# Splitting fp32 operands for one-pass matmuls: upper parts made by ScalarE instead of a VectorE mask, operands in dense blocks

## The chip, the cores and the metric

The kernel runs on one core of a Trainium2 chip. The metric is the device time of one launch in microseconds; lower is better. The core's engines are called as in the profile: PE is TensorE (PEld its weight loads), DVE is VectorE, ACT is ScalarE, POOL is GpSimd, SP is SyncE, which issues nearly all transfers.

## The reference

Four graph layers run over `x` (32 graphs of 512 nodes with 128 features) with one adjacency matrix `adj` (512 x 512) for all graphs. Each layer takes a layer norm with a relu of `x` and adds its result to `x`.

```python
h = relu(layernorm(x)); x = x + L0(h)     # graph convolution: (D^-1/2 (adj+I) D^-1/2) h W^T + b
h = relu(layernorm(x)); x = x + L1(h)     # gated graph network, five steps
h = relu(layernorm(x)); x = x + L2(h)     # graph attention, elu
h = relu(layernorm(x)); x = x + L3(h)     # graph attention

def L1_step(h):                           # in_matrix = out_matrix = adj
    m = adj @ h
    av = concat(m, m)
    z = sigmoid(av @ w3^T + h @ u3^T + b)
    r = sigmoid(av @ w4^T + h @ u3^T + b)
    hv = tanh(av @ w5^T + (r * h) @ u5^T + b)
    return (1 - z) * h + z * hv
```

The inputs and the output are fp32.

## The kernel before

**Tiling.** A graph is held as tiles of 128 partitions by 4 x 128 values: nodes on partitions in four chunks of 128 (`C = 4`), or features on partitions. Matmuls contract over partitions in chunks of 128, and products with `adj` have 512 columns.

**Products in three parts.** A matmul with fp32 operands takes two passes here (the profile counts two PE instructions for one). Products with the adjacency matrix in the gated steps (`adj`) and in most of the graph convolutions (`an`, the normalized matrix) use instead the type `float32r`, which takes one pass[...]. `in_three` splits the operand `h` in an upper part and a lower part and makes a third, `across`, from both; `factors_of` does so once for the matrix. Three one-pass products then stand for one in fp32: upper by upper and lower by lower in one PSUM bank, then a scale of the bank by 1 + 1/4096 on ACT (L630), then across by across on top (four matmuls each, L623), and a copy of the bank to `m` on ACT (L632). There are 188 such products: 160 with `adj` and 28 with `an`.

In the kernel before, the upper part begins with `cut`: DVE masks off the low 12 bits of `h` as an int32 (L613; L423 for the matrix). ACT copies `cut` to `upper` in the one-pass type (L615; L425), and DVE makes `lower` (L616; L426) and `across` (L617; L430) from `cut`. For the matrix, ACT also scales `lower` by 4096 (L428), and `across` is made from the scaled part.

**Steps and lanes.** Each graph goes through five gated steps. `step` takes `m` and the transposed state `hT`, makes the gates `r` (L729, L730, then tanh L732), `z` (L736, L738), the candidate (L743, L744, L746) and the new state (L748 to L751). Six graphs, the lanes, are under way at a time.

**Two ways to turn the state.** The new state has features on partitions; the next product needs nodes on partitions. In the first and last part of the program PE transposes it (L576) and ACT copies it (L762). In between (`EARLY <= due < STEPS * B`), `shuttle` does it: DVE transposes blocks of 32 x 32 (L584) into `sq`, four transfers write `sq` to DRAM as `far` (L587), and one reads it back as `h` (L589). In the kernel before, the shuttled state is laid out as `"(j c)"`: the values of one chunk lie four elements apart. `rows` in `in_three` then reads the matmul's weights with that stride where `turned` is true. The last step's result is added to `x` from the same layout (L766). The graphs' input to the attention layers passes through `shuttle` too, in the order `"(c j)"`.

**The order of the work.** Nothing is ordered by hand. Each operation is given to a `Plan` with its engine, an assumed cost in microseconds, a due time, and what it reads and writes. The plan plays the operations through once per trial, with a heap of ready ones for each engine and buffers taken from named pools (eight PSUM banks, two `cut`, two `upper`, two `lower`, three `across`, and so on), keeps the best trial, and emits the instructions of each engine in that order. On the chip each engine then works strictly in the order emitted. The assumed costs are the second argument of `op`, among them `V` for a DVE pass over 512 values, `A` for one on ACT, `MR` = 0.216 for a one-pass matmul of 512 columns. After `IDLE_FROM` the plan puts idle transposes (L321) where PE would rest.

Of the kernel before, what the change touches and what calls it, by code (L numbers as in the profile page):

```python
# [9 lines left out]

F32 = mybir.dt.float32
F32R = mybir.dt.float32r
I32 = mybir.dt.int32
U8 = mybir.dt.uint8
AF = mybir.ActivationFunctionType
ALU = mybir.AluOpType
# [1 line left out]
P = 128  # L18
# [4 lines left out]
Q = P // W  # L23
# [10 lines left out]

SPLIT = 4096.0
UPPER = -4096


class Val:
# [228 lines left out]
def gnn_stack(ctx: ExitStack, tc: tile.TileContext, a: dict, out: bass.AP):  # L270
# [13 lines left out]
    def flat(t):  # L284
# [110 lines left out]
    for c in range(C):  # L395
        p = Val("bank")
        turned.append(p)

        def turn_adj(c=c, p=p):
            for m in range(C):  # L400
                nc.tensor.transpose(p.t[:, m, :], adj_sb.t[:, c, m * P:(m + 1) * P], ident.t)
        op("PE", C * TURN, -800, turn_adj, r=[adj_sb[c], ident], w=[p])
        op("ACT", A, -800, lambda c=c, p=p: nc.scalar.copy(adjT.t[:, :, c * P:(c + 1) * P], p.t), r=[p], w=[adjT[c]])
# [92 lines left out]
    def norm_stats(b, due):  # L496
        xb, st, mv, ve = xs[b], Val("st", C), Val("mv"), Val("ve")
        for c in range(C):
            op("DVE", 0.21, due, lambda c=c: nc.vector.bn_stats(st.t[:, c, :], xb.t[:, c, :]), r=[xb[c]], w=[st[c]])
# [5 lines left out]
        op("DVE", 0.45, due, aggr, r=[st], w=[mv, ve])  # L505
        return mv, ve

    def norm_relu(b, y, due, times=None):
# [68 lines left out]
        op("PE", C * TURN, due, turns, r=[y, ident], w=[p, *then])  # L577
        return p

    def shuttle(src, squares, dst, due, soon, inner="(c j)"):  # L580


        sq, far = Val("sq"), Val("far", Q)
        op("DVE", 0.61, soon, lambda: nc.vector.transpose(  # L584
            sq.t.rearrange(f"p q {inner} -> p q c j", c=C), flat(src.t).rearrange(squares, c=C, q=Q)), r=[src], w=[sq])
        for k in range(Q):
            op("SP", 0.44, due, lambda k=k: nc.sync.dma_start(  # L587
                far.t[:, :, k, :].rearrange("q i f -> i q f"), sq.t[k * W:(k + 1) * W]), r=[sq], w=[far[k]], delay=4)
        op("SP", 0.4, due, lambda: nc.sync.dma_start(dst.t, far.t.rearrange("q i k f -> (q i) k f")), r=[far], w=[dst], delay=5)  # L589

    def shuttle_first(h, hT, due, soon):

        sq, far = Val("sq"), Val("far", Q)
        op("DVE", 0.61, soon, lambda: nc.vector.transpose(
            sq.t.rearrange("p k (c i) -> p k c i", c=C), h.t.rearrange("p c (k j) -> p k c j", k=Q)), r=[h], w=[sq])
        for q in range(Q):
            op("SP", 0.44, due, lambda q=q: nc.sync.dma_start(
                far.t[:, :, q, :].rearrange("k j f -> j k f"), sq.t[q * W:(q + 1) * W]), r=[sq], w=[far[q]], delay=4)
        for q in range(Q):
            op("SP", 0.4, due, lambda q=q: nc.sync.dma_start(  # L600
                hT.t.rearrange("p c (q i) -> q p c i", q=Q)[q], far.t.rearrange("k j q (c i) -> q (k j) c i", c=C)[q]),
               r=[far[q]], w=[hT[q]], delay=5)

    def in_three(h, turned, factors, due):

        cut, upper, lower, across = Val("cut"), Val("upper"), Val("lower"), Val("across")
# [4 lines left out]
        op("DVE", 0.35, due - 5, lambda: nc.vector.tensor_scalar(  # L613
            flat(cut.t).bitcast(I32), flat(h.t).bitcast(I32), UPPER, None, op0=ALU.bitwise_and), r=[h], w=[cut])
        op("ACT", A, due - 5, lambda: nc.scalar.copy(flat(upper.t), flat(cut.t)), r=[cut], w=[upper])  # L615
        op("DVE", V, due - 5, lambda: nc.vector.tensor_sub(flat(lower.t), flat(h.t), flat(cut.t)), r=[h, cut], w=[lower])  # L616
        op("DVE", V, due - 5, lambda: nc.vector.scalar_tensor_tensor(  # L617
            flat(across.t), flat(cut.t), 1 + 1 / SPLIT, flat(h.t), op0=ALU.mult, op1=ALU.subtract), r=[h, cut], w=[across])
        p, m = Val("bank"), Val("m")

        def times(left, right, first):
            for c in range(C):
                nc.tensor.matmul(flat(p.t), rows(left.t, c), right.t[:, c, :], start=first and c == 0, stop=c == C - 1,  # L623
                                 skip_group_check=True)
# [5 lines left out]
        op("ACT", A, due - 6, lambda: nc.scalar.mul(flat(p.t), flat(p.t), 1 + 1 / SPLIT), w=[p])  # L630
        op("PE", 4 * MR, due, lambda: times(across, across_of, False), r=[across, across_of], w=[p, m])
        op("ACT", A, due - 6, lambda: nc.scalar.copy(flat(m.t), flat(p.t)), r=[p], w=[m])  # L632
        return m

    def product(h, due):

        p, m = Val("bank"), Val("m")
        for c in range(C):
# [8 lines left out]
        op("ACT", A, due, lambda: nc.scalar.copy(flat(m.t), flat(p.t)), r=[p], w=[m])  # L647
        return m

    def normalized(begun):  # L650
# [56 lines left out]
    def ggnn(b, due):  # L707
# [4 lines left out]
        if FAR0 <= b < B - FAR1:  # L712
            shuttle_first(h, hT, due - 2.5, due - 3)
        else:
            p = to_features(h, due - 2, hT)
            op("ACT", A, due - 2, lambda hT=hT: nc.scalar.copy(flat(hT.t), flat(p.t)), r=[p], w=[hT])
        turned = False
        for s in range(STEPS):
            now = due + LANES * s
# [5 lines left out]
    def step(b, s, m, hT, due, lane):  # L725
# [30 lines left out]
        if not EARLY <= due < STEPS * B:  # L756
# [2 lines left out]
                op("DVE", V, due + 2, lambda: nc.vector.tensor_add(flat(xs[b].t), flat(xs[b].t), flat(p.t)),  # L759
                   r=[p, lane], w=[xs[b]])  # L760
            else:
                op("ACT", A, due + 1, lambda: nc.scalar.copy(flat(h.t), flat(p.t)), r=[p], w=[h])  # L762
            return h, False, new
        shuttle(new, "p (c q i) -> p q c i", h, due, due - 5, "(j c)")
        if last:
            op("DVE", V, due + 2, lambda: nc.vector.tensor_add(  # L766
                xs[b].t.rearrange("p c (k j) -> p k c j", k=Q), xs[b].t.rearrange("p c (k j) -> p k c j", k=Q),
                h.t.rearrange("p k (j c) -> p k c j", c=C)), r=[h, lane], w=[xs[b]])
        return h, True, new


# [25 lines left out]
    def gat(b, l, due):  # L797
# [4 lines left out]
        if near:  # L802
            rstd, g = center_relu(b, y, due), Val("off", 2)
            pT = to_features(y, due + 1, gT)
            op("ACT", A, due + 1, lambda: nc.scalar.copy(flat(gT.t), flat(pT.t)), r=[pT], w=[gT])
        else:
            norm_relu(b, y, due)
            shuttle(y, "p (c q j) -> p q c j", gT, due + 0.5, due)
# [47 lines left out]
            op("SP", 0.4, due + 1.5, lambda: nc.sync.dma_start(  # L856
                row.t, line.t.rearrange("c q i -> (c q i)").unsqueeze(0).to_broadcast([P, N])), r=[line], w=[row, e], delay=7)
        for j in range(C):
            op("DVE", 0.68, due + 3, lambda j=j: nc.vector.scalar_tensor_tensor(  # L859
                e.t[:, j, :], matrix(row), h.t[:, j, D + 1:D + 2], mask.t[:, j, :], op0=ALU.max, op1=ALU.mult),  # L860
               r=[row, h[2 + j // 2], mask], w=[e[j]])

# [112 lines left out]
```

## Time and profile before

| | us |
|---|---|
| median of 3 runs | 1607.32 (1606.89 to 1607.37) |
| the profiled execution's own time | 1608.62 |
| span of the profiled execution | 1606.8 |
| PE busy | 1589.5 |
| PE weight loads busy (overlap PE) | 1160.8 |
| DVE busy | 1481.0 |
| ACT busy | 905.6 |
| POOL busy | 152.5 |

The span runs from the first to the last instruction on the core; the time of a run has a little around it. Busy times are of one profiled execution. A row of a group gives the line, engine, operation, the tiles out<-in, the shape, the count, then busy microseconds in total and the mean nanoseconds of one, then the idle time of the engine just before those instructions and what ended it.

### The profile page before, as it was taken

To read this page: it belongs to the slowest core of one execution; us is meant where nothing else is said; L and a number is where in the kernel's file an instruction comes from. 1 tells how busy PE (TensorE), PEld (TensorE's weight loads), DVE (VectorE), ACT (ScalarE), POOL (GpSimd) and SP (SyncE) were. 2 spreads that over 40 slices of the span, in tenths; PEclk is the share of its full clock that TensorE was granted. 3 is DMA by queue.
4 is the path that set the end of the run, shared out by engine and by line. 5 is a ranking of instruction groups with operands and counts; after the bars stand their busy time and mean duration, and the time that the engine had idled before them with its cause. 6 is when DMAs were issued, how large, how long until landed. Compare 5 with 4: busy or idle time off the path is not lost.

```text
span 1606.8 us, 23090 instructions
## 1 busy us (share of the span) xinstructions
PE 1589.5 (99%) x6966; PEld 1160.8 (72%) x6966; DVE 1481.0 (92%) x3751; ACT 905.6 (56%) x1822; POOL 152.5 (9%) x137
## 2 busy tenths in 40 slices
PE   8899999999999999999999999999999999999998
PEld 7576667776777776777777686777676766767678
DVE  8989789999999999999999999999999899987888
ACT  6765555555555545645555645655655555555464
POOL 2111000000100101010110110101010000000010
PEclk9999999999999999999999999999999999999999
DMA  3134233444543443444433534444344424432201
GB/s 105 33 86 110 64 95 97 116 115 113 126 103 101 105 119 92 109 114 120 117 100 93 125 102 122 109 102 112 87 124 116 110 71 106 115 100 66 53 27 41
DMA packets 270141, 157.66 MB, mean 98 GB/s; under 512 B 81248, under 2 KB 236224, under 8 KB 270016
## 3 DMA queue, kind: packets, MB, share of 16 engines
q1 hardware_dynamic: 269728, 155.66, 38.0%
q8 instruction: 55, 0.90, 0.2%
q14 instruction: 70, 0.57, 0.1%
q10 hardware_dynamic: 288, 0.52, 0.1%
HBM read 86.25 MB, written 69.84 MB: 97 GB/s over the span
## 4 chain that ended last, share of the span: by engine, by line
PE 90%; DVE 7%; ACT 1%; issue 1%; POOL 0%; DMA 0%; DVEq 0%; ACTq 0%; POOLq 0%
PE bank L623 32%; PE bank L885 11%; PE bank L729 8%; PE bank L730 8%; PE bank L743 8%; PE bank L744 8%; PE bank L736 8%; PE bank L818 3%; PE bank L693 2%; PE bank L871 1%; DVE sq L584 1%; DVE e L859 1%; PE bank L576 0%; DVE hT L751 0%; DVE hv L748 0%
## 5 line engine op out<-in xcount | busy, mean ns | idle before, releaser
L512 POOL TENSOR_TENSOR rstd<-ve,mhalf 128x4 f32<-128x4 f32 x119 | 140.8, 1184 | 1366.1 <-DVE ve L504 1161.8
L885 PEld LDWEIGHTS bank<-h_gat,e 128*128 128x128 f32 x1792 | 210.5, 191 | 17.9 <-issue 14.4
L623 PE MATMUL bank<-adj,across 128*128 128x512 f32 x640 | 215.3, 462 | 1.6 <-ACT bank L630 1.6
L630 ACT ACTIVATE bank<-bank 128x512 f32<-128x512 f32 x188 | 109.3, 581 | 186.2 <-PE bank L623 183.6
L885 PE MATMUL bank<-h_gat,e 128*128 128x129 f32 x1792 | 212.2, 275 | 0.3 <-DVE v L890 0.3
L623 PE MATMUL bank<-adj,upper 128*128 128x512 f32 x640 | 201.2, 436 | 1.3 <-ACT upper L615 1.3
L623 PEld LDWEIGHTS bank<-adj,across 128*128 128x128 f32 x640 | 156.2, 280 | 41.6 <-issue 22.4
L732 ACT ACTIVATE r<-bank,gate_bw 128x512 f32<-128x512 f32 x160 | 109.7, 686 | 127.3 <-PE bank L730 118.4
L623 PE MATMUL bank<-adj,lower 128*128 128x512 f32 x640 | 177.0, 398 | 0.0
L623 PEld LDWEIGHTS bank<-adj,upper 128*128 128x128 f32 x640 | 154.4, 280 | 30.1 <-issue 8.8
L729 PE MATMUL bank<-m,wT 128*128 128x512 f32 x320 | 164.4, 595 | 3.0 <-ACT m L632 2.5
L736 PE MATMUL bank<-m,wT 128*128 128x512 f32 x320 | 163.4, 594 | 1.8 <-ACT r L732 1.8
L743 PE MATMUL bank<-m,wT 128*128 128x512 f32 x320 | 163.8, 593 | 0.7 <-DVE h_gat L836 0.6
L744 PE MATMUL bank<-rh,wT 128*128 128x512 f32 x320 | 163.5, 592 | 0.7 <-DVE rh L734 0.7
L584 DVE STREAM_TRANSPOSE sq<-hT 128x512 f32<-128x512 f32 x148 | 163.6, 1105 | 0.2
L730 PE MATMUL bank<-hT,wT 128*128 128x512 f32 x320 | 163.4, 592 | 0.0
L746 ACT ACTIVATE hv<-bank,gate_bw 128x512 f32<-128x512 f32 x160 | 109.5, 684 | 93.9 <-PE bank L744 93.0
L623 PEld LDWEIGHTS bank<-adj,lower 128*128 128x128 f32 x640 | 152.9, 280 | 7.2
L859 DVE SCALAR_TENSOR_TENSOR e<-row,h_gat,maskT 128x512 f32<-128x512 f32 x224 | 156.4, 740 | 0.0
L748 DVE TENSOR_TENSOR hv<-hv,hT 128x512 f32<-128x512 f32 x160 | 109.6, 686 | 42.4 <-ACT hv L746 41.9
L615 ACT CAST upper<-cut 128x512 fp32r<-128x512 f32 x188 | 115.2, 613 | 45.7 <-DVE cut L613 44.3
L632 ACT COPY m<-bank 128x512 f32<-128x512 f32 x188 | 109.9, 586 | 53.8 <-PE bank L623 53.3
(155 smaller groups left out, 2504.5 us busy)
## 6 DMA issues: line engine op xcount, KB each, us to landing
far<-sq SPq DMA_DIRECT2D x928, 64.0 KB
h<-far SPq DMA_DIRECT2D x148, 256.0 KB
gT<-far SPq DMA_DIRECT2D x56, 256.0 KB
row<-line SPq DMA_DIRECT2D x56, 256.0 KB
hT<-far SPq DMA_DIRECT2D x112, 64.0 KB
x<-in_x_dram SPq DMA_DIRECT2D x24, 256.0 KB
out_dram<-x SPq DMA_DIRECT2D x20, 256.0 KB
adjT<-in_x_dram SPq DMA_DIRECT2D x8, 256.0 KB
```

The source lines that it names most:

```text
L512: op("POOL", 1.0, due, lambda: nc.gpsimd.tensor_tensor(rstd.t, ve.t, mhalf.t, ALU.pow), r=[ve, mhalf], w=[rstd])
L584: op("DVE", 0.61, soon, lambda: nc.vector.transpose(sq.t.rearrange(f"p q {inner} -> p q c j", c=C), flat(src.t).rearrange(squares, c=C, q= ...
L615: op("ACT", A, due - 5, lambda: nc.scalar.copy(flat(upper.t), flat(cut.t)), r=[cut], w=[upper])
L623: nc.tensor.matmul(flat(p.t), rows(left.t, c), right.t[:, c, :], start=first and c == 0, stop=c == C - 1, skip_group_check=True)
L632: op("ACT", A, due - 6, lambda: nc.scalar.copy(flat(m.t), flat(p.t)), r=[p], w=[m])
L729: nc.tensor.matmul(flat(gate.t), gates.t[:, 0, :], flat(m.t), start=True, stop=False)
L730: nc.tensor.matmul(flat(gate.t), gates.t[:, 1, :], flat(hT.t), start=False, stop=True)
L736: op("PE", MM, due + 0.3, lambda: nc.tensor.matmul(flat(gate.t), gates.t[:, 2, :], flat(m.t), start=False, stop=True, skip_group_check=Tru ...
L743: nc.tensor.matmul(flat(cand.t), gates.t[:, 3, :], flat(m.t), start=True, stop=False)
L744: nc.tensor.matmul(flat(cand.t), u5T.t[:, 0, :], flat(rh.t), start=False, stop=True)
L859: op("DVE", 0.68, due + 3, lambda j=j: nc.vector.scalar_tensor_tensor(e.t[:, j, :], matrix(row), h.t[:, j, D + 1:D + 2], mask.t[:, j, :], ...
L885: nc.tensor.matmul(pt()[:, c, :D + 1], e.t[:, j, i * P:(i + 1) * P], h.t[:, j, :D + 1], start=(j == 0), stop=(j == C - 1))
```

## The change

ACT makes `upper` straight from `h`: it scales by 1 - 2**-13[...]. There is no mask, and the `cut` tiles are gone. DVE makes `lower` from `h` and `upper`, and `across` from `lower` and `upper`. Of the matrix the same is done, and `across` is made from the unscaled `lower`. The shuttled state keeps the order `"(c j)"`; where it is turned, `upper` and `lower` are read from `h` in runs of 32 values and written in dense chunks, so that the matmuls read dense weights. Several of the planner's assumed costs are other numbers.

```diff
 SPLIT = 4096.0
-UPPER = -4096
+BELOW = 1 - 2.0 ** -13
...
-        "cut": tiles(2, TOKENS, "cut"),
...
-    V, A = 0.61, 0.585
+    V, A, COPY = 0.595, 0.575, 0.495
...
         for c in range(C):
-            cut = Val("cut")
-            op("DVE", 0.35, due, lambda c=c, cut=cut: nc.vector.tensor_scalar(
-                flat(cut.t).bitcast(I32), mT.t[:, c, :].bitcast(I32), UPPER, None, op0=ALU.bitwise_and), r=[mT], w=[cut])
-            op("ACT", A, due, lambda c=c, cut=cut: nc.scalar.copy(upper.t[:, c, :], flat(cut.t)), r=[cut], w=[upper[c]])
-            op("DVE", V, due, lambda c=c, cut=cut: nc.vector.tensor_sub(
-                lower.t[:, c, :], mT.t[:, c, :], flat(cut.t)), r=[mT, cut], w=[lower[c]])
-            op("ACT", A, due, lambda c=c: nc.scalar.mul(
+            op("ACT", COPY, due, lambda c=c: nc.scalar.mul(upper.t[:, c, :], mT.t[:, c, :], BELOW), r=[mT], w=[upper[c]])
+            op("DVE", V, due, lambda c=c: nc.vector.tensor_sub(
+                lower.t[:, c, :], mT.t[:, c, :], upper.t[:, c, :].bitcast(F32)), r=[mT, upper[c]], w=[lower[c]])
+            op("DVE", V, due, lambda c=c: nc.vector.scalar_tensor_tensor(
+                across.t[:, c, :], upper.t[:, c, :].bitcast(F32), -1 / SPLIT, lower.t[:, c, :].bitcast(F32),
+                op0=ALU.mult, op1=ALU.add), r=[lower[c], upper[c]], w=[across[c]])
+            op("ACT", COPY, due, lambda c=c: nc.scalar.mul(
                 lower.t[:, c, :], lower.t[:, c, :].bitcast(F32), SPLIT), w=[lower[c]])
-            op("DVE", V, due, lambda c=c, cut=cut: nc.vector.tensor_sub(
-                across.t[:, c, :], lower.t[:, c, :].bitcast(F32), flat(cut.t)), r=[lower[c], cut], w=[across[c]])
...
-    def shuttle(src, squares, dst, due, soon, inner="(c j)"):
+    def shuttle(src, squares, dst, due, soon):
...
-        op("DVE", 0.61, soon, lambda: nc.vector.transpose(
-            sq.t.rearrange(f"p q {inner} -> p q c j", c=C), flat(src.t).rearrange(squares, c=C, q=Q)), r=[src], w=[sq])
+        op("DVE", 0.617, soon, lambda: nc.vector.transpose(
+            sq.t.rearrange("p q (c j) -> p q c j", c=C), flat(src.t).rearrange(squares, c=C, q=Q)), r=[src], w=[sq])
...
-        def rows(t, c):
-            return t.rearrange("p k (j c) -> p c (k j)", c=C)[:, c] if turned else t[:, c, :]
-        op("DVE", 0.35, due - 5, lambda: nc.vector.tensor_scalar(
-            flat(cut.t).bitcast(I32), flat(h.t).bitcast(I32), UPPER, None, op0=ALU.bitwise_and), r=[h], w=[cut])
-        op("ACT", A, due - 5, lambda: nc.scalar.copy(flat(upper.t), flat(cut.t)), r=[cut], w=[upper])
-        op("DVE", V, due - 5, lambda: nc.vector.tensor_sub(flat(lower.t), flat(h.t), flat(cut.t)), r=[h, cut], w=[lower])
+        if turned:
+            def given(t):
+                return t.rearrange("p k (c j) -> p c k j", c=C)
+
+            def made(t):
+                return t.rearrange("p c (k j) -> p c k j", k=Q)
+        else:
+            given = made = flat
+        op("ACT", COPY, due - 5, lambda: nc.scalar.mul(made(upper.t), given(h.t), BELOW), r=[h], w=[upper])
+        op("DVE", V, due - 5, lambda: nc.vector.tensor_sub(made(lower.t), given(h.t), made(upper.t).bitcast(F32)),
+           r=[h, upper], w=[lower])
         op("DVE", V, due - 5, lambda: nc.vector.scalar_tensor_tensor(
-            flat(across.t), flat(cut.t), 1 + 1 / SPLIT, flat(h.t), op0=ALU.mult, op1=ALU.subtract), r=[h, cut], w=[across])
+            flat(across.t), flat(lower.t).bitcast(F32), -SPLIT, flat(upper.t).bitcast(F32), op0=ALU.mult, op1=ALU.add),
+           r=[lower, upper], w=[across])
...
-                nc.tensor.matmul(flat(p.t), rows(left.t, c), right.t[:, c, :], start=first and c == 0, stop=c == C - 1,
+                nc.tensor.matmul(flat(p.t), left.t[:, c, :], right.t[:, c, :], start=first and c == 0, stop=c == C - 1,
...
-        shuttle(new, "p (c q i) -> p q c i", h, due, due - 5, "(j c)")
+        shuttle(new, "p (c q i) -> p q c i", h, due, due - 5)
         if last:
             op("DVE", V, due + 2, lambda: nc.vector.tensor_add(
                 xs[b].t.rearrange("p c (k j) -> p k c j", k=Q), xs[b].t.rearrange("p c (k j) -> p k c j", k=Q),
-                h.t.rearrange("p k (j c) -> p k c j", c=C)), r=[h, lane], w=[xs[b]])
+                h.t.rearrange("p k (c j) -> p k c j", c=C)), r=[h, lane], w=[xs[b]])
```

The assumed costs changed besides: copies and scales on ACT from `A` to `COPY`, the block transposes from 0.61 to 0.617, `bn_stats` from 0.21 to 0.192, the aggregation after it from 0.45 to 0.33, and the `e` pass of the attention (L859) from 0.68 to 0.65.

More of the change, by code (lines that the diff above doesn't have):

```diff
@@ L12 @@
 F32R = mybir.dt.float32r
-I32 = mybir.dt.int32
 U8 = mybir.dt.uint8
@@ L402, in gnn_stack @@
         op("PE", C * TURN, -800, turn_adj, r=[adj_sb[c], ident], w=[p])
-        op("ACT", A, -800, lambda c=c, p=p: nc.scalar.copy(adjT.t[:, :, c * P:(c + 1) * P], p.t), r=[p], w=[adjT[c]])
+        op("ACT", COPY, -800, lambda c=c, p=p: nc.scalar.copy(adjT.t[:, :, c * P:(c + 1) * P], p.t), r=[p], w=[adjT[c]])
         if c % 2 == 0:
@@ L498, in norm_stats @@
         for c in range(C):
-            op("DVE", 0.21, due, lambda c=c: nc.vector.bn_stats(st.t[:, c, :], xb.t[:, c, :]), r=[xb[c]], w=[st[c]])
+            op("DVE", 0.192, due, lambda c=c: nc.vector.bn_stats(st.t[:, c, :], xb.t[:, c, :]), r=[xb[c]], w=[st[c]])
         def aggr():
@@ L504, in aggr @@
             nc.vector.tensor_scalar_add(ve.t, mv.t[:, :, 1], EPS)
-        op("DVE", 0.45, due, aggr, r=[st], w=[mv, ve])
+        op("DVE", 0.33, due, aggr, r=[st], w=[mv, ve])
         return mv, ve
@@ L593, in shuttle_first @@
         sq, far = Val("sq"), Val("far", Q)
-        op("DVE", 0.61, soon, lambda: nc.vector.transpose(
+        op("DVE", 0.617, soon, lambda: nc.vector.transpose(
             sq.t.rearrange("p k (c i) -> p k c i", c=C), h.t.rearrange("p c (k j) -> p k c j", k=Q)), r=[h], w=[sq])
@@ L604, in in_three @@
     def in_three(h, turned, factors, due):
[L608 removed]
+        upper, lower, across = Val("upper"), Val("lower"), Val("across")
         upper_of, lower_of, across_of = factors
[L611 to L616 removed]
+        if turned:
[8 more added lines that the diff above has]
+           r=[h, upper], w=[lower])
         op("DVE", V, due - 5, lambda: nc.vector.scalar_tensor_tensor(
[L618 removed]
+            flat(across.t), flat(lower.t).bitcast(F32), -SPLIT, flat(upper.t).bitcast(F32), op0=ALU.mult, op1=ALU.add),
+           r=[lower, upper], w=[across])
         p, m = Val("bank"), Val("m")
@@ L629, in in_three @@
         op("PE", 8 * MR, due, first_two, r=[upper, lower, upper_of, lower_of], w=[p])
-        op("ACT", A, due - 6, lambda: nc.scalar.mul(flat(p.t), flat(p.t), 1 + 1 / SPLIT), w=[p])
+        op("ACT", COPY, due - 6, lambda: nc.scalar.mul(flat(p.t), flat(p.t), 1 + 1 / SPLIT), w=[p])
         op("PE", 4 * MR, due, lambda: times(across, across_of, False), r=[across, across_of], w=[p, m])
-        op("ACT", A, due - 6, lambda: nc.scalar.copy(flat(m.t), flat(p.t)), r=[p], w=[m])
+        op("ACT", COPY, due - 6, lambda: nc.scalar.copy(flat(m.t), flat(p.t)), r=[p], w=[m])
         return m
@@ L646, in product @@
             op("PE", MM, due, times, r=[h[c], adjT, diag[c]], w=[p, m])
-        op("ACT", A, due, lambda: nc.scalar.copy(flat(m.t), flat(p.t)), r=[p], w=[m])
+        op("ACT", COPY, due, lambda: nc.scalar.copy(flat(m.t), flat(p.t)), r=[p], w=[m])
         return m
@@ L715, in ggnn @@
             p = to_features(h, due - 2, hT)
-            op("ACT", A, due - 2, lambda hT=hT: nc.scalar.copy(flat(hT.t), flat(p.t)), r=[p], w=[hT])
+            op("ACT", COPY, due - 2, lambda hT=hT: nc.scalar.copy(flat(hT.t), flat(p.t)), r=[p], w=[hT])
         turned = False
@@ L761, in step @@
             else:
-                op("ACT", A, due + 1, lambda: nc.scalar.copy(flat(h.t), flat(p.t)), r=[p], w=[h])
+                op("ACT", COPY, due + 1, lambda: nc.scalar.copy(flat(h.t), flat(p.t)), r=[p], w=[h])
             return h, False, new
-        shuttle(new, "p (c q i) -> p q c i", h, due, due - 5, "(j c)")
+        shuttle(new, "p (c q i) -> p q c i", h, due, due - 5)
         if last:
@@ L804, in gat @@
             pT = to_features(y, due + 1, gT)
-            op("ACT", A, due + 1, lambda: nc.scalar.copy(flat(gT.t), flat(pT.t)), r=[pT], w=[gT])
+            op("ACT", COPY, due + 1, lambda: nc.scalar.copy(flat(gT.t), flat(pT.t)), r=[pT], w=[gT])
         else:
@@ L858, in gat @@
         for j in range(C):
-            op("DVE", 0.68, due + 3, lambda j=j: nc.vector.scalar_tensor_tensor(
+            op("DVE", 0.65, due + 3, lambda j=j: nc.vector.scalar_tensor_tensor(
                 e.t[:, j, :], matrix(row), h.t[:, j, D + 1:D + 2], mask.t[:, j, :], op0=ALU.max, op1=ALU.mult),
```

## Prediction

> **What bounds the kernel now.** I read the page's busy shares first, then the chain that ended last, then the busy time by stretches of the span, and only then single lines.
>
> ```profile
> span 1606.8 us, 23090 instructions
> ...
> PE 1589.5 (99%) x6966; PEld 1160.8 (72%) x6966; DVE 1481.0 (92%) x3751; ACT 905.6 (56%) x1822; POOL 152.5 (9%) x137
> ...
> PEclk9999999999999999999999999999999999999999
> ...
> PE 90%; DVE 7%; ACT 1%; issue 1%; POOL 0%; DMA 0%; DVEq 0%; ACTq 0%; POOLq 0%
> PE bank L623 32%; PE bank L885 11%; PE bank L729 8%; PE bank L730 8%; PE bank L743 8%; PE bank L744 8%; PE bank L736 8%; PE bank L818 3%; PE bank L693 2%; PE bank L871 1%; DVE sq L584 1%; DVE e L859 1%; PE bank L576 0%; DVE hT L751 0%; DVE hv L748 0%
> ```
>
> PE is busy 99% of the span, at the full granted clock, and holds 90% of the chain; a third of that is L623, the three-part products. DVE at 92% is close behind, yet has only 7% of the chain. The busy time by stretches says where that is:
>
> ```profile
> 0.00:50.00 50.00, 41.66 (x217) 32.53 (x218) 42.42 (x164) 33.44 (x72) 10.72 (x16) 1.00 0.31 85
> ...
> 1500.00:1607.00 107.00, 101.66 (x691) 86.10 (x689) 92.42 (x292) 53.54 (x152) 9.78 (x9) 1.00 0.13 38
> ```
>
> (length, then PE, PEld, DVE and ACT busy.) Of PE's 17.3 us idle, 8.3 fall before 50 us and 5.3 after 1500 us; all the rest has 3.7. So in the 1450 us between, an edit is worth what it takes off PE's own work, and DVE or ACT work taken away is worth nothing unless it ends one of those few waits. A busy PE isn't a PE at its peak, however, so I looked inside L623. By source line, count, then ns min/median/max:
>
> ```profile
> L623 PEld LDWEIGHTS bank<-adj,upper x640: 186/309/332, 32.8 to 1540.5; 128*128 128x128 f32 x160
> L623 PEld LDWEIGHTS bank<-adj,lower x640: 187/310/313, 33.6 to 1541.4; 128*128 128x128 f32 x160
> ...
> L623 PEld LDWEIGHTS bank<-an,upper x112: 186/188/192, 62.1 to 1245.9; 128*128 128x128 f32 x112
> ```
>
> A weight load takes 188 ns from a dense operand (all of `an`, and `adj` in untransposed steps) and 310 ns from an operand whose rows lie four elements apart (`rows` with `turned`). The timeline prices this. First a dense stretch, then a strided one (start, length; L623 blocks of four matmuls follow each other):
>
> ```profile
> 78.66 1.10 PE L623 MATMUL bank<-adj,upper 128*128 128x512 f32 x4
> ...
> 84.27 0.94 PE L693 MATMUL bank<-wT,m 128*128 128x128 f32 x7
> ```
>
> ```profile
> 1391.75 1.06 PE L818 MATMUL bank<-w_aug,gT 128*128 128x131 f32 x8
> 1392.56 1.31 PE L623 MATMUL bank<-adj,upper 128*128 128x512 f32 x4
> 1393.70 1.12 PE L623 MATMUL bank<-adj,lower 128*128 128x512 f32 x4
> ...
> 1399.40 1.02 PE L729 MATMUL bank<-m,wT 128*128 128x512 f32 x2
> ```
>
> Dense: six blocks in 5.61 us, 0.935 each. Strided: the last six of seven blocks in 5.70 us, 0.950 each; the first, which follows short matmuls of some 112 ns, takes 1.14. Its dense equal (an L693 row at 170.00, blocks at 170.81, 171.83, 172.77) takes 1.02.
>
> **What the skill says.** The Trainium skill, "Advanced Engine Details and Errata", SBUF Cachelines: SBUF has 16-byte lines, and accesses that each touch another line pay. The trace agrees: four f32 apart is a new line each time, and 188 ns becomes 310. "TensorE: Matmul & The Clock Gate", Back-to-back issue gap: the spacing of matmuls comes from load and matmul together, pipelined. Agreed in kind: a load 120 ns longer costs only 4 ns per matmul (0.950 against 0.935 per four) behind a 512-column matmul, but the whole 120 ns behind a 112 ns one. "VectorE: DVE Perf Modes", TRN2 errata: an fp32 two-operand pass over 512 elements takes 691 ns; L616 here has 683. "Perfetto Trace Analysis", Identifying the Most-Contended Engine: judge TensorE by weight-load share too; it is 72% here, so loads can matter.
>
> **The change, part by part.**
>
> *Dense split operands.* All 120 transposed steps are concerned: 148 `h<-far` transfers less the 28 that end in L766. That is 1440 of L623's 2256 matmuls, 360 blocks of four. Going through the trace's list of matmuls I count 36 blocks that begin behind a short matmul: 36 x 0.125 = 4.5 us (1167 against 1042 ns for a lone block between short and long ones). The other 324 save 0.015 to 0.017 each: 5.2 us. All of it is PE's own work in a PE-bound stretch: **-9.7 us**. Dense blocks showed no such dependence on what precedes them, so a new order of PE can't lose this.
>
> *DVE.* These rows carry the price (busy us, mean ns):
>
> ```profile
> L584 DVE STREAM_TRANSPOSE sq<-hT 128x512 f32<-128x512 f32 x148 | 163.6, 1105 | 0.2
> L613 DVE TENSOR_SCALAR cut<-h 128x512 int32<-128x512 int32 x160 | 66.5, 416 | 1.3 <-ACT upper L615 0.4 <-ACT h L518 0.3 <-ACT h L762 0.2
> L584 DVE STREAM_TRANSPOSE sq<-y 128x512 f32<-128x512 f32 x56 | 39.4, 704 | 5.7 <-ACT y L518 5.6
> L766 DVE TENSOR_TENSOR x<-x,h 128x512 f32<-128x512 f32 x20 | 21.8, 1091 | 0.0
> ```
>
> 188 masks at 0.416 go (78 us), and 8 for the factors (3 us). The 148 transposes, which wrote with a stride of 16 bytes, take the y form, 0.704: 59 us. The 28 residual adds read densely: 28 x (1.091 - 0.684) = 11 us. DVE falls from 1481 to about 1330 us, 83%. Between 50 and 1500 us PE covers all of this; worth at most the 3.7 us of idle there. I take **-0.5**.
>
> *ACT.* `upper` is read from `h` in 32-element runs and scaled. The trace has no such form: at best it costs 0.58 (the scale of L630), at worst what stride did to the transposes, 0.61 x 1.57 = 0.96, 42 us more over 120 steps. I take 0.63, as L428 writes the one-pass type. Even the worst leaves ACT below 60%, covered by PE. The reads of `lower` in the same runs lie between 0.684 and L766's 1.09; at worst 49 us come back to DVE, still below before. I take 0.70, since the y transposes walk such runs at 0.704.
>
> *The waits.* Before, `cut` on DVE waited for the landed `h`, and ACT for `cut` (44.3 us in 43 waits, off the chain). Now `upper` on ACT waits for the landing and `lower` on DVE waits for `upper`, so the tanh of other lanes queue behind a late `h` on ACT. To the first block, mask plus copy (0.34 + 0.1 + 0.61) becomes one ACT pass, 0.4 us earlier; `lower`, needed 0.93 later, is ready in time. `across` needs `lower` too, but feeds the third block only, after 1.9 us of PE and the 0.58 of L630. In the factors `across` no longer waits for the scaled `lower`.
>
> *Start and end.* The chain of waits in the first 50 us holds L423 three times (0.34 and 0.67 us), L613 once (0.34), and L428 (0.54) ahead of L430; all go or leave the path: 1.9 us. DVE's new wait for ACT gives some back: **-1.5**. The end is products, softmax and `e` on DVE (L859), which the edit doesn't touch: 0.
>
> *Planner.* DVE, ACT and SP emit the same work less the masks, SP still 1462 issues, so no queue gains a transfer; the planner's costs change, so every engine's order does. The idle transposes fall from 20 to 11, which costs and gains nothing: they fill gaps. The new costs (0.595 for a DVE pass, 0.495 for a copy) lie nearer to the start-to-start distances in the trace (0.60, 0.50); the transposes were planned at 0.61 and came 0.94 to 1.0 apart, and now match. I price the order at 0 with -2 to +10 as bounds.
>
> Sum: -9.7 - 1.5 - 0.5 = -11.7 us against the profiled span of 1606.8 (that run's time was 1608.6; the median of the runs is 1607.3, so 1.3 us under it). I subtract from the median: **1595.5 us**.
>
> **Rivals.** A difference under 0.2%, 3.2 us, is about what a measurement of this kernel can't tell from none.
> - *Half of it.* The 4 ns per matmul come from something else, such as where the operands lie, and only the 36 short cases (4.5) and the start count: 1602. Against: dense and strided blocks differ alike at 80 us and at 1390 us.
> - *More.* The lighter DVE also removes most of the 3.7 us in the middle and 5 of the 8.3 at the start: 1607.3 - 9.7 - 3 - 5, about 1588. For: DVE is in the chain just there.
> - *Slower.* ACT's in-order queue stops at `upper` until `h` has landed. Before, DVE reached its `cut` so late that it shows no wait for a DMA (L613's idle is 1.3 us, none from a DMA); ACT, idle 44% of the time, may come sooner. It decides once the 120 landings pass on more than (11.7 + 3.2) / 120 = 0.12 us each to PE; at 0.17 each, 20 us: 1615. Against: PE runs 0.234 us per matmul where the plan assumes 0.216, so landings come early by the plan; and six lanes are in flight. For: all orders are new.
>
> **Chances.** As reckoned 0.66 (1589 to 1601), half 0.11 (of which 0.05 within 0.2%), more 0.11, slower 0.12 (0.01 of it within 0.2%). So faster 0.83, same 0.06, slower 0.11. The range takes in the half case and the nearer part of the larger gain, with the order's bounds: 1585 to 1605.
>
> **What would show it.** Right: no LDWEIGHTS of L623's successor above 200 ns; blocks 0.935 apart; transposes all near 0.70 and no int32 row; DVE near 1330 us, PE busy near 1581 with idle near 15. Wrong: PE idle well above 17 us with ACT `upper` or a tanh as releaser, or ACT waiting for `h<-far`; or strided reads of `upper` near 1 us; or weight loads that stay at 310.

## The result, and the profile after

The changed kernel takes 1589.04 us (median of 4 runs, 1588.57 to 1590.1) against 1607.34 us: a ratio of 0.9886, 95% interval 0.9869 to 0.9903. That is 18.3 us less, where 11.8 were forecast. The time lies in the range; the gain is 1.55 times the forecast.

From the page after, the span, the engines' busy shares and the chain that ended last:

```profile
span 1588.3 us, 22967 instructions
...
PE 1575.3 (99%) x6957; PEld 1079.2 (68%) x6957; DVE 1371.1 (86%) x3555; ACT 904.8 (57%) x1822; POOL 150.0 (9%) x137
...
PE 89%; DVE 8%; ACT 1%; DMA 1%; issue 1%; SPq 0%; POOL 0%; DVEq 0%; POOLq 0%; ACTq 0%
```

PE still bounds the kernel. Its weight loads are 82 us less busy, DVE is 110 us less, ACT the same. By stretches (length, then PE, PEld, DVE and ACT busy), first the two that were shown of before:

```profile
0.00:50.00 50.00, 46.05 (x235) 35.64 (x235) 42.39 (x168) 37.17 (x78) 11.84 (x17) 1.00 0.30 85
...
1500.00:1589.00 89.00, 82.65 (x606) 71.78 (x604) 80.85 (x271) 46.06 (x139) 9.69 (x9) 1.00 0.14 40
```

PE's idle time fell from 8.3 to 3.95 us in the first 50 us and stayed between 5 and 6.5 at the end. The weight loads, by source line (count, ns min/median/max):

```profile
L626 PEld LDWEIGHTS bank<-adj,upper x640: 186/188/192, 31.2 to 1526.0; 128*128 128x128 f32 x160
L626 PEld LDWEIGHTS bank<-adj,lower x640: 187/188/189, 32.1 to 1526.9; 128*128 128x128 f32 x160
```

Not one of 2256 is long any more. And the groups of DVE and ACT that changed (busy us, mean ns of one | idle before):

```profile
L619 DVE SCALAR_TENSOR_TENSOR across<-lower,upper 128x512 fp32r<-128x512 f32 x188 | 126.6, 674 | 2.4 <-PE bank L626 2.1
L617 DVE TENSOR_TENSOR lower<-h,upper 128x512 fp32r<-128x512 f32 x160 | 108.8, 680 | 24.9 <-ACT upper L616 23.4 <-issue 0.3
L581 DVE STREAM_TRANSPOSE sq<-hT 128x512 f32<-128x512 f32 x148 | 103.7, 701 | 0.4
L616 ACT ACTIVATE upper<-h 128x512 fp32r<-128x512 f32 x160 | 99.7, 625 | 10.5 <-DVE across L619 5.8 <-PE bank L626 3.5 <-ACT bank L633 0.2
L769 DVE TENSOR_TENSOR x<-x,h 128x512 f32<-128x512 f32 x20 | 13.6, 680 | 0.0
```

The new wait is there, `lower` for ACT's `upper` (23.4 us), but it hardly reaches PE: L626 sat idle for `lower` 0.5 us in all, and for `upper` 0.5 us. ACT waits for no landed `h`; its one wait for a transfer is 1.2 us, for the matrix at the start.

**One account for all runs.** PE's busy time hides short gaps, since the ends of matmuls are modelled. So I took every distance from one matmul's start to the next and subtracted what such a step takes undisturbed: 429 ns for 512 fp32 columns, 233 for a dense one-pass matmul, 112 for 128 columns. What is over in a run of L623 matmuls without a stall is the cost of long loads; a larger excess is a wait. It was summed by stretches of the span (us). Where such a step is set a few ns higher or lower, the levels from 100 to 1500 us move by 2 to 4 us, in all runs alike; so differences between runs are what the account gives, and small ones with care.

| | before | after | difference | forecast |
|---|---|---|---|---|
| long weight loads | 10.3 | 0.2 | -10.1 | -9.7 |
| PE waits from 20 to 100 us | 10.4 | 3.8 | -6.6 | -1.5 |
| PE waits from 100 to 1500 us | 7.8 | 6.2 | -1.6 | -0.5 |
| PE waits after 1500 us | 3.9 | 4.6 | +0.7 | 0 |
| first 20 us | 4.5 | 4.7 | +0.2 | 0 |
| idle transposes (20, then 11) | | | -1.0 | 0 |

It sums to -18.4; the spans differ by 18.5. The loads came as forecast, so the questions were: where do the 6.6 us at the start come from, and is the middle as indifferent to DVE as the forecast had it?

### The profile page after: what moved, and what is told of

Same layout as the page of the kernel before. It is cut to its first block, busy times and chain, and to the rows that moved or that the text cites. A ratio compares the mean times of both kernels' runs of the same rounds, so it can differ in the third digit from the quotient of the medians.

```text
span 1588.3 us, 22967 instructions
## 1 busy us (share of the span) xinstructions
PE 1575.3 (99%) x6957; PEld 1079.2 (68%) x6957; DVE 1371.1 (86%) x3555; ACT 904.8 (57%) x1822; POOL 150.0 (9%) x137
## 4 chain that ended last, share of the span: by engine, by line
PE 89%; DVE 8%; ACT 1%; DMA 1%; issue 1%; SPq 0%; POOL 0%; DVEq 0%; POOLq 0%; ACTq 0%
PE bank L626 31%; PE bank L888 12%; PE bank L739 8%; PE bank L746 8%; PE bank L747 8%; PE bank L732 8%; PE bank L733 8%; PE bank L821 3%; DVE e L862 2%; PE bank L696 1%; PE bank L874 1%; DVE st L496 0%; DVE x L898 0%; DVE across L619 0%; POOL rstd L509 0%
## 5 line engine op out<-in xcount | busy, mean ns | idle before, releaser
L626 PE MATMUL bank<-adj,across 128*128 128x512 f32 x640 | 214.1, 459 | 0.0
L626 PE MATMUL bank<-adj,upper 128*128 128x512 f32 x640 | 198.1, 431 | 0.1
L626 PE MATMUL bank<-adj,lower 128*128 128x512 f32 x640 | 175.1, 395 | 0.0
L626 PEld LDWEIGHTS bank<-adj,across 128*128 128x128 f32 x640 | 118.3, 189 | 62.3 <-issue 42.1
L626 PEld LDWEIGHTS bank<-adj,upper 128*128 128x128 f32 x640 | 119.0, 188 | 50.0 <-issue 21.4
L741 ACT ACTIVATE z<-bank,gate_bw 128x512 f32<-128x512 f32 x160 | 109.3, 683 | 66.2 <-PE bank L739 61.1
L626 PEld LDWEIGHTS bank<-adj,lower 128*128 128x128 f32 x640 | 120.2, 188 | 28.8
L515 ACT ACTIVATE y<-x,off,rstd 128x128 f32<-128x128 f32 x252 | 110.2, 487 | 38.1 <-DVE off L512 35.4
```

The source lines that it names most:

```text
L515: op("ACT", 0.385, due, lambda c=c: nc.scalar.activation(chunk(y, c), xb.t[:, c, :], AF.Relu, bias=off.t[:, c:c + 1], scale=rstd.t[:, c:c ...
L626: nc.tensor.matmul(flat(p.t), left.t[:, c, :], right.t[:, c, :], start=first and c == 0, stop=c == C - 1, skip_group_check=True)
```

## The experiments

Three things changed: masks gone (M), operands dense (D), assumed costs new (C). Since only M and C enter the plan's reckoning, a kernel with D alone keeps the order of the kernel before on every engine. All eight combinations of the three were measured, so each part can be read with the others present or absent; where M or C changes, the plan makes a new order, and its effect is in the difference too. "Gap" is DVE's busy time less the sum of the costs that the plan holds for DVE, both in us. In four runs a number at the start holds a stretch of PE at half clock besides waits; it is given under "The start".

| run | what it has | median us | ratio to before, interval | long loads | PE waits 20 to 100 | 100 to 1500 | gap |
|---|---|---|---|---|---|---|---|
| before | | 1607.3 | | 10.3 | 10.4 | 7.8 | 58 |
| e1_dense | D | 1591.5 | 0.9902, 0.9888 to 0.9915 | -0.3 | 10.4 | 2.8 | 12 |
| e12_no_masks_only | M | 1598.4 | 0.9940, 0.9926 to 0.9954 | 8.7 | 7.8 | 4.2 | 69 |
| e4_new_costs | C | 1621.0 | 1.0085, 1.0072 to 1.0099 | 8.8 | 10.6 | 21.3 | 102 |
| e3_old_costs | M, D | 1586.9 | 0.9870, 0.9854 to 0.9885 | -0.3 | 8.6 | 1.7 | 20 |
| e2_strided | M, C | 1614.9 | 1.0048, 1.0035 to 1.0060 | 8.6 | 3.9 | 23.4 | 119 |
| e5_dense_new_costs | D, C | 1593.4 | 0.9910, 0.9897 to 0.9924 | -0.4 | 9.3 | 2.4 | 54 |
| after | M, D, C | 1589.0 | 0.9886, 0.9869 to 0.9903 | 0.2 | 3.8 | 6.2 | 64 |
| e6_dve_load | after, DVE burdened | 1610.5 | 1.0018, 1.0012 to 1.0025 | 0.6 | 3.9 | 26.0 | 126 |
| e7_strided_priced | M, C, stride priced | 1598.1 | 0.9940, 0.9928 to 0.9953 | 10.6 | 3.9 | 3.3 | 54 |
| e9_padded | after, in e7's order | 1588.0 | 0.9879, 0.9864 to 0.9894 | 0.1 | 3.5 | 3.3 | 1 |
| e8_mr | after, true PE cost | 1590.0 | 0.9891, 0.9876 to 0.9906 | 0.5 | 5.7 | 5.9 | 62 |
| e10_factor_masks | after, masks in factors | 1592.6 | 0.9908, 0.9893 to 0.9923 | 0.2 | 9.0 | 5.1 | 62 |
| e11_step_masks | after, masks in steps | 1589.2 | 0.9886, 0.9870 to 0.9903 | -0.2 | 8.2 | 4.0 | 55 |

### Dense blocks alone (e1_dense)

```diff
-            return t.rearrange("p k (j c) -> p c (k j)", c=C)[:, c] if turned else t[:, c, :]
+                return t.rearrange("p k (c j) -> p c k j", c=C)
...
-                nc.tensor.matmul(flat(p.t), rows(left.t, c), right.t[:, c, :], start=first and c == 0, stop=c == C - 1,
+                nc.tensor.matmul(flat(p.t), left.t[:, c, :], right.t[:, c, :], start=first and c == 0, stop=c == C - 1,
...
-        shuttle(new, "p (c q i) -> p q c i", h, due, due - 5, "(j c)")
+        shuttle(new, "p (c q i) -> p q c i", h, due, due - 5)
```

> The kernel before with dense operand blocks alone: masks, ACT copies and all assumed costs stay, and every engine keeps the order of the kernel before. (Where `across` can't be made in one DVE instruction from `cut` and `h`, it is made from `cut` and `lower`, or in 21 of 120 steps by four short instructions.) Theory (weight loads cost PE 9.7 us, the rest of the gain is PE waiting less in the first 100 us): no L623 load above 200 ns, waits of PE in the first 100 us unchanged at about 15 us, time 1607.3 - 9.7 = 1597.6, between 1596 and 1599. Rival (the gain comes from a lighter DVE and a new order, and long loads were hidden): 1605 to 1607. Second rival (a lighter DVE also removes the waits at the start): 1592 or less.

1591.5 us: 15.7 less, not 9.7. The order is the same and the start is unchanged to a tenth (10.4 us of waits), so all of it lies in the steady part. The loads gave 10, and PE's waits from 100 to 1500 us fell from 7.8 to 2.8. Those 5 us are DVE's doing: the same order, on an engine that ran the 148 transposes in 699 ns in place of 1105. The theory was right on the loads and the start, and wrong that the middle doesn't feel DVE. The second rival had the time and the engine but the wrong place.

### The stride put back (e2_strided)

The reverse of that edit, on the changed kernel.

> The changed kernel with the four-element stride put back (transposes, weights and residual adds as before), in the changed kernel's order on every engine, with no masks. Theory: loads of the transposed steps return to 310 ns and PE gains 9 to 10 us of work: 1589.0 + 9.7 = 1598.7, between 1597 and 1600.5; PE's waits in the first 100 us stay near 8.5 us. Rival (DVE's 70 us are what counts): PE idle above 20 us in the middle, 1603 or more. Rival (loads hidden in this order): below 1592.

1614.9 us, slower than the kernel before, and 25.8 more than the changed kernel, which has the same order. Long loads are 8.4 us of it; PE's waits in the middle rose by 17.2, from 6.2 to 23.4. The loads alone explain a third. The rival with DVE came true, both in the waits and in the time.

### DVE burdened, loads dense (e6_dve_load)

```diff
+            if extra:
+                nc.vector.tensor_add(waste, flat(src.t)[:, :384], flat(src.t)[:, :384])
```

> The changed kernel, order and dense operands untouched, with one useless DVE addition over 384 elements after each of the 148 transposes of the state, of which the plan knows nothing: some 0.46 us each, 69 us of DVE in all, as much as the stride cost it. Theory D: no load is longer, yet PE waits after 100 us rise from 11 us (end included) to about 28 as in the strided run of this order: 1589 + 17 = 1606, between 1601 and 1610. Rival (in the strided run the long loads themselves made the waits): below 1595.

1610.5 us, 21.5 more than the changed kernel. Not a load is longer, the order is the same, and the waits in the middle went from 6.2 to 26.0. From its groups, the useless addition beside the transposes:

```profile
L585 DVE STREAM_TRANSPOSE sq<-hT 128x512 f32<-128x512 f32 x148 | 103.7, 701 | 0.4
L588 DVE TENSOR_TENSOR waste<-hT 128x384 f32<-128x384 f32 x148 | 76.2, 515 | 0.0
```

And by stretches, 400 to 1200 us, this kernel and then the changed one (length, then PE, PEld, DVE busy):

```profile
400.00:800.00 400.00, 398.01 (x1717) 267.65 (x1717) 364.40 (x924) 220.89 (x441) 37.42 (x32) 1.00 0.42 109
800.00:1200.00 400.00, 396.18 (x1704) 264.91 (x1703) 363.41 (x935) 220.54 (x437) 38.83 (x33) 1.00 0.41 107
```

```profile
400.00:800.00 400.00, 400.00 (x1747) 273.30 (x1746) 351.10 (x883) 223.60 (x444) 35.94 (x31) 1.00 0.43 110
800.00:1200.00 400.00, 400.00 (x1770) 274.51 (x1769) 356.68 (x923) 225.25 (x448) 40.22 (x34) 1.00 0.43 110
```

DVE at 91% of the stretch makes PE wait; at 88 to 89% it doesn't. But the kernel before ran there with DVE still busier and PE full:

```profile
400.00:800.00 400.00, 399.90 (x1730) 293.82 (x1728) 377.15 (x955) 226.13 (x450) 40.38 (x34) 1.00 0.43 110
800.00:1200.00 400.00, 399.81 (x1735) 293.50 (x1734) 380.91 (x950) 226.82 (x450) 39.28 (x33) 1.00 0.42 108
```

So the share is not the measure. What differs is what the plan knew. Nor did the long loads of e2_strided make its waits: per us that DVE is busier than in the changed kernel, PE waits 0.31 us more there (17.2 of 54.9) and 0.32 here (19.8 of 62.0), with no long load.

### The stride priced (e7_strided_priced)

```diff
-        op("DVE", 0.617, soon, lambda: nc.vector.transpose(
+        op("DVE", 0.97 if inner == "(j c)" else 0.617, soon, lambda: nc.vector.transpose(
...
-            op("DVE", V, due + 2, lambda: nc.vector.tensor_add(
+            op("DVE", 1.0, due + 2, lambda: nc.vector.tensor_add(
```

> The strided run (no masks, stride put back, 1614.9) with two assumed costs set to what the trace shows for the strided forms: 0.97 for the transpose of the state and 1.0 for the residual add, so that the plan makes another order. Theory D in its narrow form (what hurts is a cost the plan doesn't know): PE waits after 100 us fall from 28 us to 12 or less, 1596 to 1602 with the long loads. Rival (88% of DVE busy is too much in any order): 1610 or more.

1598.1 us. Two assumed costs took 16.7 us off e2_strided with the same work on every engine (nine idle transposes more on PE), in another order: the waits in the middle fell from 23.4 to 3.3, with DVE as busy as there (1424.9 against 1426.0 us). What hurts is DVE work that the plan doesn't know of, not the work. The narrow form of the theory held. That an order alone, good by chance, made the difference is answered below by pairs of runs in one order (e12_no_masks_only).

### The costs (e3_old_costs, e4_new_costs, e5_dense_new_costs, e8_mr)

```diff
-    V, A, COPY = 0.595, 0.575, 0.495
+    V, A, COPY = 0.61, 0.585, 0.585
```

> The changed kernel with all assumed costs of the planner as before (0.61 a DVE pass, 0.585 an ACT pass and copy, 0.61, 0.21, 0.45, 0.68), so a third order. Theory S (the start is shorter because eight masks and a dependence of the factors went): the first 100 us keep about 8.5 us of PE waits, 1588 to 1591. Theory C (the costs set the order that lets the second graph's first product come early): the waits at the start return to 13 us or more, 1593 to 1596.

> The kernel before (masks, stride) with the changed kernel's assumed costs alone. Theory S: the waits at the start stay near 15 us, 1606 to 1608. Theory C: they fall to about 9 us, 1600 to 1603.

Neither theory on the start held in both runs. With the old costs the start was 8.6 us although the masks had gone (6.9 of it waits, the rest half clock), between the two forecasts, and yet the run came out at 1586.9, because the middle fell to 1.7. With the new costs alone the start stayed at 10.6 (9.3 of it waits), as theory S had it, but the middle rose to 21.3, which neither foresaw. The new costs, true for dense forms, are the worse ones while the stride is there (+13.7 us): the old ones charged each pass and statistic somewhat too much, and so covered part of what the transposes cost beyond their 0.61.

> Masks kept, new assumed costs (the order of the run with new costs alone, 1621.0), operands in dense blocks as in the dense run. Theory D (a plan's order holds only while DVE is as light as the plan assumed; strided transposes and adds are some 70 us more than planned): the dense blocks take off the 8.8 us of weight loads and most of the 21 us of PE waits after 100 us: 1621 - 9 - 15 = 1597, between 1593 and 1600. Rival (this order is simply a bad one): only the weight loads go, 1611 or more.

1593.4 us: the same order as e4_new_costs, 27.6 us less, of which 9 are loads and 19 waits in the middle. As the theory had it.

> The changed kernel with the assumed cost of a one-pass matmul set to the 0.234 us that the trace shows, in place of 0.216. If true costs always make the better order: 1583 to 1588, with less than 6 us of PE waits between 20 and 1500 us. If a plan that thinks PE faster than it is serves as slack for DVE and ACT: 1589 to 1597.

1590.0 us, the same within its interval. The first answer failed: 11.6 us of waits between 20 and 1500 us, not under 6. The second isn't shown, as its range holds the changed kernel's own 1589.0: a true cost for PE changed nothing that can be measured.

### DVE ahead of its plan (e9_padded)

The costs of e7_strided_priced, in the changed kernel.

> The changed kernel, dense, its instructions unchanged, but planned as if the transposes of the state cost 0.97 and the residual adds 1.0: every engine has the order of the run with priced stride (1598.1), in which DVE is now some 70 us lighter than the plan thinks. Theory (DVE ahead of its plan leaves PE no waits in the middle): 1598.1 less 10.3 us of long loads and less 2 to 3 of the 3.3 us of PE waits from 100 to 1500 us: 1585.3, between 1584 and 1587, with PE waits of 3.9 us between 20 and 100 us. Rival (the load on DVE is what counts, and below some 88% the order doesn't matter): as the changed kernel, 1588 to 1590.

1588.0 us: 1 us under the changed kernel where 3.7 were expected, with intervals that overlap; the rival had the time. The loads went as expected, but the waits of the middle are at 3.3 as in e7_strided_priced, so in this order a gap of 1 us gave no more than one of 54. The pair also prices the loads apart from DVE: one order, equal waits in the middle, 10.5 us of long loads less by the account, and 10.15 us less in the time of the runs.

### The start (e10_factor_masks, e11_step_masks)

The masked form of `factors_of`, or of `in_three`, in the changed kernel. In these two the scales of the two `across` operands don't match, so their third product lacks its proper scale; that is a matter of values, and leaves the instructions and their shapes as they would be in a matching pair.

> The changed kernel with the masks put back in the eight blocks of the matrix factors only (and `across` of the factors made from the scaled lower part again); the steps stay without masks; costs as in the changed kernel, order made anew. Theory F (the shorter start comes from the factors): PE waits from 20 to 100 us rise from 3.8 to 8 us or more, 1592 to 1595. Theory S (it comes from the steps): 5 us or less there, 1588 to 1591.

> The mirror image: masks in the 188 splits of the steps (dense blocks), none in the factors; costs as in the changed kernel, order made anew. Theory F: PE waits from 20 to 100 us stay at 5 us or less, 1587 to 1590. Theory S: 8 us or more, 1592 to 1594. Neither, if both runs lie between: then the order that the two make together decides.

Factor masks alone brought the start to 9.0, step masks alone to 8.2, both (e5_dense_new_costs) to 9.3. But these numbers need one correction. In four of the profiled executions the granted clock of PE fell to 0.50 for 3.4 us after one of its long waits: from 26.6 us in e12_no_masks_only, 38.9 in e4_new_costs, 42.0 in e3_old_costs and 52.4 in e11_step_masks. Steps took about twice as long there (853 ns for 429, 427 for 233). The stretch from 39 to 42 us, in e4_new_costs and then in e5_dense_new_costs, which has the same order (the clock stands third from the end):

```profile
39.00:42.00 3.00, 2.94 (x4) 1.17 (x4) 2.97 (x11) 2.16 (x5) 0.11 (x1) 0.50 0.00 0
```

```profile
39.00:42.00 3.00, 1.98 (x4) 0.68 (x4) 2.97 (x11) 2.78 (x6) 0.00 (x0) 1.00 0.00 0
```

The half clock is 1.3 us of the start of e4_new_costs and 1.6 to 1.7 of the others, so that their waits are 6.2 (e12), 9.3 (e4), 6.9 (e3) and 6.6 us (e11). The kernel before, the changed kernel and e10_factor_masks have no such stretch.

So theory F comes nearer. Factor masks cost 5.2 us at the start and 3.6 in time (1592.6), both as F had it; with step masks the time is 1589.2, again as F had it, and the waits of 6.6 us lie between the forecasts. The masks are not the whole of it: without any, but with old costs, the waits are 6.9 and 6.2 us, not 3.8. What the good order does is seen in PE's timeline, before and then after (start, length; the wait and its releaser in brackets):

```profile
31.88 1.16 PE L693 MATMUL bank<-wT,m 128*128 128x128 f32 x8
32.79 1.18 PE L623 MATMUL bank<-adj,upper 128*128 128x512 f32 x4
33.81 1.10 PE L623 MATMUL bank<-adj,lower 128*128 128x512 f32 x4
35.58 1.20 PE L623 MATMUL bank<-adj,across 128*128 128x512 f32 x4 [0.67 <-ACT bank L630]
37.51 1.12 PE L729 MATMUL bank<-m,wT 128*128 128x512 f32 x2 [0.73 <-ACT m L632]
38.47 1.02 PE L730 MATMUL bank<-hT,wT 128*128 128x512 f32 x2
39.33 0.60 PE L576 MATMUL bank<-ident,h 128*128 128x128 f32 x4
```

```profile
32.27 1.10 PE L626 MATMUL bank<-adj,lower 128*128 128x512 f32 x4
33.21 1.05 PE L696 MATMUL bank<-wT,m 128*128 128x128 f32 x8
34.27 0.66 PE L573 MATMUL bank<-ident,h 128*128 128x128 f32 x4
34.68 1.18 PE L626 MATMUL bank<-adj,across 128*128 128x512 f32 x4
35.70 1.10 PE L626 MATMUL bank<-adj,upper 128*128 128x512 f32 x4
36.63 1.10 PE L626 MATMUL bank<-adj,lower 128*128 128x512 f32 x4
```

Before, PE follows the first graph's chain alone and waits at each link; the second graph's `h` is transposed at 39.33. After, other work stands between the links, and the second graph arrives at 34.27. On DVE its `off` comes at 30.35 instead of 36.59, as the work ahead of it, the additions to `x` among it, stands earlier in DVE's order (27.19 against 33.23):

```profile
33.23 1.12 DVE L697 SCALAR_TENSOR_TENSOR x<-bank,dinv,x 128x128 f32<-128x128 f32 x4
...
36.59 0.15 DVE L515 SCALAR_TENSOR_TENSOR off<-mv,rstd 128x4 f32<-128x4 f32 x1
```

```profile
27.19 1.11 DVE L700 SCALAR_TENSOR_TENSOR x<-bank,dinv,x 128x128 f32<-128x128 f32 x4
...
30.35 0.16 DVE L512 SCALAR_TENSOR_TENSOR off<-mv,rstd 128x4 f32<-128x4 f32 x1 [0.24 <-POOL rstd L509]
```

Why the plan finds this order with both sets of masks gone and these costs, and not otherwise, was not settled.

### No masks and nothing else (e12_no_masks_only)

> The masks gone and nothing else: operands strided, all assumed costs as before, in the order of the run with old costs (1586.9) on every engine. Theory (PE's waits in the middle follow the gap between DVE's busy time and the sum of its assumed costs): the plan holds 1354 us for DVE, the strided forms bring it to some 1429, a gap of 75 us, between the changed kernel (64 us, 6.2 us of PE waits from 100 to 1500 us) and the run with new costs alone (102 us, 21 us). So 9 to 13 us of waits in place of 1.7, and 10 us of long loads: 1586.9 + 9 + 9 = 1605, between 1602 and 1608, no faster than the kernel before by more than 5 us. Rival (masks were 80 us of DVE, so their absence alone brings most of the gain): 1599 or less.

1598.4 us, 9.0 less than before, and the rival's number. The waits in the middle are 4.2 us at a gap of 69. So the gap is no fine measure: all runs below 70 us have 1.7 to 7.8 us of waits in no clear order, the three above 100 have 21 to 26. Nothing was tried between. Pairs in one order agree, and leave the order out of it: a gap that grows from 12 to 58, from 20 to 69 or from 1 to 54 us costs 5.0, 2.5 and 0 us of waits (e1_dense and before, e3_old_costs and e12_no_masks_only, e9_padded and e7_strided_priced); from 54 to 102, or from 64 to 119 or 126, it costs 18.9, 17.2 and 19.8 (e5 and e4, the changed kernel and e2 or e6).

### What each part is worth

From the eight combinations: dense blocks take off 15.8 us alone, 11.5 with masks gone, 27.6 with new costs, 25.8 with both. Masks gone: 9.0 alone, 4.6 with dense, 6.1 with new costs, 4.4 with both. New costs add 13.7 us alone, 16.5 without masks, and 2 with dense blocks. The changed kernel without its new costs, e3_old_costs, has the lowest time of all kernels (0.9870 against 0.9886 of before). All its runs (1585.3 to 1587.0) lie below those of the changed kernel (1588.6 to 1590.1), but the intervals of the ratios overlap, so it isn't shown to be better.

## Why the prediction was right, and where it was off

The main term, dense weights, was right, and the range held. The gain beyond it was forecast at 2.0 us and came to some 8, from two terms that were too small; 1589.0 lies at the very edge of what was called "as reckoned" (1589 to 1601). That it lies inside is luck as much as reckoning.

- **Dense split operands, -9.7 us.** Right in mechanism and size: 10.1 by the account, and no load above 192 ns. Pricing a strided block from the timeline, apart for blocks behind short matmuls, was what made this term exact. The pair e7_strided_priced and e9_padded confirms it by the times of runs.
- **"Between 50 and 1500 us PE covers all of this; worth at most the 3.7 us of idle there. I take -0.5."** This is the term mis-sized most in the steady part. With the order unchanged (e1_dense) a lighter DVE took off 5.0 us of waits. Two things were wrong. The 3.7 us came from PE's busy share, which hides short gaps; from the starts of matmuls the waits were 7.8. And DVE was taken as covered because it was off the chain; it ran at 94 to 95% from 400 to 1200 us. In the changed kernel only 1.6 of the 5 us remain, as its own order has more waits.
- **"Start and end", -1.5 us.** Mis-sized: -6.6 us. The masks gone, with old costs, took off 3.5 us of waits (10.4 to 6.9, dense in both) or 4.2 (e12_no_masks_only), and each time a new order came with it; the rest, some 3 us, is the order that the new costs make.
- **Planner, "I price the order at 0 with -2 to +10".** The bounds held for the sum: from e1_dense, in the order of before, to the changed kernel it is 2.4 us less, masks included. But 0 stood for two larger parts of either sign: the start fell by 6.6 us, the middle rose by 3.4 (2.8 to 6.2).
- **DVE "to about 1330 us".** 1371. Mean durations of neighbours overlap: a mask lasts 0.416 us but starts 0.334 before the next instruction, a strided transpose 1.105 against 0.94. Sums of durations overstate what an engine is freed of: 152 us by durations, some 124 from start to start, 110 measured. The last difference was not traced.
- **The waits, ACT, `lower`.** Right: `upper` takes 0.625 where 0.63 was taken, `lower` 0.680 in runs of 32 where 0.70 was, and no tanh is held up by a late `h`. "Slower" didn't come about. What could have made a change like this slower is shown by e2_strided: DVE work missing from the plan, which no rival named.
- **"More"** (1588) had the time nearly right, and the size of the start, but not its cause: a lighter DVE alone left the start at 10.4 us (e1_dense).
- **Sums.** The terms give 1595.6, not 1595.5; those of "Half" 1601.3, not 1602; those of "More" 1589.6, not 1588, so that it hardly differed from the lower end of "as reckoned".

Why the changed kernel's middle has 6.2 us of waits where e1_dense has 2.8 and e3_old_costs 1.7 was not traced to single instructions.

## What to carry to other kernels

A stride of four fp32 values was paid three times here: by the transpose that writes it (1105 ns against 701), by the addition that reads it (1091 against 680), and by the weight load (310 against 188). The transpose in between was the place to put the order right. Where an order is planned ahead from assumed costs, an operation that takes longer than assumed can make the bounding engine wait, though its own engine has room: in the changed kernel's order, 55 to 62 us more of DVE work of which the plan knew nothing cost 17 to 20 us of waits on PE, and telling the plan of it, in e7_strided_priced, took the waits below those of the changed kernel. Change a form and its assumed cost together, and judge cover by the starts on the bounding engine, not by its busy share.

## What was not expected of the hardware

- A long wait of PE can cost more than itself. Four profiled executions show the granted clock at 0.50 for 3.4 us after a wait of 1.7 to 2.4 us, which costs 1.3 to 1.7 us more. It doesn't always come: after the same wait of 2.3 us, in the same order, e4_new_costs has it and e5_dense_new_costs doesn't. Differences of under 2 us between kernels are of this size.
- The first 20 us vary by some 2 us between profiled executions with the same instructions in the same order. Waits for the rows of `adj` are one part of it. Another is that short matmuls step at 213 ns there before they step at 111: the change comes at 5.9 us in e7_strided_priced and at 10.7 us in e9_padded, which have one order, and makes 1.7 us between them. It comes when the trace's record of the granted clock begins.
- Reading in runs of 32 values (128 bytes) is free: `upper` on ACT takes 0.625 us so, and 0.625 from a flat `h` in e2_strided; `lower` on DVE 0.680 against 0.683.
